# A graph network on one core: one gathered row in each gather is stored to DRAM, and edge step 1 loads its features four steps ahead

## The chip, the cores and the metric

The kernel runs on one core of a Trainium2 chip. The metric is the device time of one execution in microseconds (us). Engines are named as in the profile: PE (matmul; PEld is its weight load), DVE, ACT, POOL and SP. POOL issues the indirect transfers (gathers), SP and ACT issue the ordinary ones; a "q" behind an engine's name stands for its queue of issued transfers.

## The reference

A graph of 12,500 nodes and 412,500 edges, sorted by destination, passes through two networks, each added to x and followed by a layer norm. The first is a two-layer graph convolution. The second, which the change touches, is a mesh network with D = 64 features:

```
n = ln(mlp(node_feat)); e = ln(mlp(edge_feat))
for s in range(2):
    ce = concat([e, n[senders], n[receivers]])
    e  = e + ln(mlp_s(ce))                       # mlp: silu(x @ w0 + b0) @ w1 + b1
    agg = segment_sum(e, receivers)
    n  = n + ln(mlp_node_s(concat([n, agg])))
return mlp(n)
```

## The kernel before, in words

Sorting, the graph convolution and the node encoder run first (to about 5405 us). Then `edge_step(s)` runs twice, for s = 0 (about 5405 to 10757 us) and s = 1 (10777 to 15661 us). Each goes over 405 groups of K = 8 times 128 edges, written out as one straight line of code.

The product of n[senders] with its part of w0 is taken once per node and lies in DRAM as a table, tab_p; n[receivers] as tab_q. Per group:

- `ahead(g)` (L1028) gathers 8 x 128 rows of tab_p on POOL: eight instructions (L407, one per k), each 128 rows of 64 floats, into buffer g % R of `ring`, five buffers pg0 to pg4. It is called LA = 3 groups ahead of the block that reads it, and three times ahead of the loop.
- `send(g)` (L1012) loads, on SP, what the group starts from: in s = 0 the raw edge attributes `at` (L960, two buffers), in s = 1 the edge features e that s = 0 stored (L1018, six buffers).
- `send_window` brings the receivers' window: qd, rows of tab_q (L1045), and rb, relative places (L1041), in four parts. For groups 0 and 1 SP issues them, for all others ACT, between its activations. `hot` (L1050, DVE) turns rb into a one-hot.
- `hidden_enc` (s = 0 only: matmul L965, silu L967) is the edge encoder's first layer. `hidden_blk` adds up in PSUM the product with e and with the one-hot window (L974) and the transposed gathered rows (L976), and ACT takes the silu (L979). `second` (L984, L986) is the second layer, `normalised` the layer norm (DVE L466, L471, and ACT L465), `window_sum` the segment sum (PE L389, then DVE L397).
- s = 0 stores the new e (L1110, SP).

Block g and the parts behind it lie in different steps of the loop (a step is one turn of `for g` in `steps`): in s = 0 encoder, its second layer, its turning, block, second layer and sum are 0 to 5 steps behind, in s = 1 block, second layer and sum 0 to 2. In 25 of the steps a chunk of nodes is updated in between (L926 loads its degrees, L906 and L908 send new tables in s = 0).

The order of PE, DVE and ACT is that of the program text (`manual_schedule`). SP's and POOL's order is the scheduler's, from what each instruction waits for. Engines wait for each other by semaphores. A gather into a ring buffer waits until PE has read the buffer's last contents, five groups before (L976).

Of the kernel before, what the change touches and what calls it, by code (L numbers as in the profile page):

```python
# [9 lines left out]
F32 = mybir.dt.float32  # L10
# [8 lines left out]
P = 128  # L19
K = 8  # L20
W = 64
D = 64
GB = 135
SI, DR = 81, 45
R, LA = 5, 3
# [12 lines left out]
def gcn_then_mesh_gnn_kernel(ctx: ExitStack, tc: tile.TileContext, a: dict, out: bass.AP):  # L38
# [21 lines left out]
    nc = tc.nc  # L60
# [3 lines left out]
    NG = NT // K  # L64
# [6 lines left out]
    KP = K // 2  # L71
    assert N == NB * NP and NB == NCH * CB and NT == IT * TB == ITS * TI

    dram = ctx.enter_context(tc.tile_pool(name="dram", bufs=1, space=bass.MemoryType.DRAM))
# [45 lines left out]
    tabs_p = [dram.tile([N, D], F32, name=f"tab_p{s}") for s in range(2)]  # L120
    tabs_q = [dram.tile([N + 1, D], F32, name=f"tab_q{s}") for s in range(2)]
    tabs_q3 = [dram.tile([N + W, 3, D], BF16, name=f"tab_q3{s}") for s in range(2)]
    e1_d = dram.tile([128, NG * KP * P], F32, name="e1_d")

    def bank(name):
# [84 lines left out]
    with tc.tile_pool(name="sort", bufs=1) as sp, \  # L210
# [7 lines left out]
        k, other = keys  # L218
# [82 lines left out]
        k, free = keys[turn], keys[1 - turn]  # L301
# [102 lines left out]
    def gather(table, idx, to):  # L404

        for k in range(K):
            nc.gpsimd.indirect_dma_start(  # L407
                out=to[:, k, :], out_offset=None, in_=table,
                in_offset=bass.IndirectOffsetOnAxis(ap=idx[:, k:k + 1], axis=0))
# [587 lines left out]
    def edge_step(s):  # L997


        ring = [work.tile([P, K, D], F32, name=f"pg{i}", bufs=1) for i in range(R)]  # L1000
        acc = (s01, 0, 128) if s == 0 else (ns2, D, D)

        ENC, ENC2, TURN, BLK, BLK2, SUM = (0, 1, 2, 3, 4, 5) if s == 0 else (None, None, None, 0, 1, 2)
        CHUNK = 4
        nh = work.tile([D, CN + P - NP], F32, name="nh", bufs=1)
        nc.vector.memset(nh, 0.0)
        feats, hids, hidb, y0, y1, es, windows, hots, ohs, srcs, drls, ny, dh = ({} for _ in range(13))
        col = lambda g: slice(g * KP * P, (g + 1) * KP * P)
        real = lambda g: 0 <= g < NG
        chunk_at = {last_group[c] + SUM + 1: c for c in range(NCH)}  # L1010

        def send(g):  # L1012

            if s == 0:
                feats[g] = edge_inputs(g * KP * P)
            else:
                es[g] = work.tile([128, KP * P], F32, name="e", bufs=6)
                nc.sync.dma_start(es[g], e1_d[:, col(g)])  # L1018

        def send_sources(i):  # L1020
            srcs[i] = work.tile([P, SI * K], I32, name="si")
            nc.sync.dma_start(srcs[i], a["srcT"][:, i * SI * K:(i + 1) * SI * K])

        def send_places(i):
            drls[i] = work.tile([P, DR * K], F32, name="drl")
            nc.sync.dma_start(drls[i], rel_d[:, i * DR * K:(i + 1) * DR * K])

        def ahead(g):  # L1028
            at = g % SI * K
            gather(tabs_p[s], srcs[g // SI][:, at:at + K], ring[g % R])  # L1030

        def send_window(g, eng=nc.sync, parts=range(4)):

            if 0 in parts:
                windows[g] = qd[g % len(qd)], work.tile([128, KP * P], BF16, name="rb", bufs=3)
            q, rb = windows[g]
            for i in parts:
                h = i // 2
                r = slice(h * W, (h + 1) * W)
                if i % 2:  # L1040
                    eng.dma_start(rb[r, :], relg_d[g:g + 1, h, :].to_broadcast([W, KP * P]))  # L1041
                else:
                    at = nc.values_load(base_row[0:1, g:g + 1], engines=[eng.engine], min_val=0, max_val=N,
                                        skip_runtime_bounds_check_because="a destination is a node's number or N")
                    eng.dma_start(q[r, :, h * D:(h + 1) * D], tabs_q3[s][ds(at, W)])  # L1045

        def hot(g):
            q, rb = windows.pop(g)
            ot = work.tile([128, KP * P], BF16, name="ot")
            nc.vector.tensor_scalar(ot, rb, iop, None, op0=OP.is_equal)  # L1050
            hots[g] = [(q[:, i, :], ot) for i in range(3)]

        def steps():
            for g in range(2):
                send(g)
                send_window(g)
            hot(0)
            later = []
            for g in range(NG + SUM + 1 + CHUNK):
                if real(g + 2):  # L1060
                    send(g + 2)
                if g + 8 - SUM >= 0 and real(g + 8 - SUM) and (g + 8 - SUM) % DR == 0:
                    send_places((g + 8 - SUM) // DR)
                if real(g - BLK + LA) and g >= BLK:
                    if (g - BLK + LA + 8) % SI == 0 and real(g - BLK + LA + 8):
                        send_sources((g - BLK + LA + 8) // SI)
                    ahead(g - BLK + LA)

                def window_part(i):
                    if real(g - BLK + 2) and g - BLK >= 0:  # L1070
                        send_window(g - BLK + 2, nc.scalar, [i])


                while later:
                    later.pop(0)()

                if real(g - SUM + 1):
                    c = g - SUM + 1
                    ohs[c] = one_hot(work, drls[c // DR], c % DR)
                if real(g - BLK + 1) and g - BLK >= 0:  # L1080
                    hot(g - BLK + 1)

                parts = []
                if s == 0 and real(g - ENC2):
                    c = g - ENC2
                    y0[c] = work.tile([P, K, D], F32, name="y0", bufs=5)
                    parts.append((second(hids.pop(c), *ee1), y0[c]))
                if real(g - BLK2):
                    c = g - BLK2
                    y1[c] = work.tile([P, K, D], F32, name="y")  # L1090
                    parts.append((second(hidb.pop(c), *eb1[s]), y1[c]))
                if g - 1 in chunk_at:
                    c = chunk_at[g - 1]
                    ny[c] = work.tile([P, CB, D], F32, name="ny", bufs=1)
                    parts.append((node_second(nh, *nb1[s], n=P, name="seg"), ny[c]))
                if parts:
                    normalised(work, P, *parts)
                window_part(0)
                if s == 0 and real(g - TURN):
                    c = g - TURN  # L1100
                    es[c] = work.tile([128, KP * P], F32, name="e", bufs=6)
                    nc.scalar.activation(es[c], turned(y0[c]), AF.Identity, scale=e_g[0])
                window_part(1)
                if real(g - SUM):
                    c = g - SUM
                    y, e = [y1.pop(c)], es.pop(c)
                    if s == 0:
                        later.append(lambda c=c, e=e, pt=turned(y[0]): (
                            nc.vector.scalar_tensor_tensor(e, pt, e_g[1], e, op0=OP.mult, op1=OP.add),
                            nc.sync.dma_start(e1_d[:, col(c)], e)))  # L1110
                        y.insert(0, y0.pop(c))
                    window_sum(ohs.pop(c), base_row, c, lambda k: [v[:, k, :] for v in y], *acc, later)
                if s == 0 and real(g):
                    hids[g] = hidden_enc(feats.pop(g))
                window_part(2)
                if real(g - BLK):
                    c = g - BLK
                    hidb[c] = hidden_blk(s, es[c], ring[c % R], hots.pop(c))
                window_part(3)

                if g in chunk_at:
                    node_hidden(step_products(s, chunk_at[g]), nb_b0[s], nh)
                if g - 2 in chunk_at:
                    c = chunk_at[g - 2]
                    step_update(s, c, node_turned(ny.pop(c)))
                if g - 3 in chunk_at:
                    c = chunk_at[g - 3]
                    if s == 0:
                        send_tables(1, c)
                    else:  # L1130
                        dh[c] = decode_hidden(c)
                if s and g - 4 in chunk_at:
                    c = chunk_at[g - 4]
                    decode_second(c, dh.pop(c))

        with tc.For_i(0, trip_count(0, 1)):
            send_sources(0)
            send_places(0)
            for g in range(LA):
                ahead(g)  # L1140
            with tc.manual_schedule(engines={ET.PE, ET.DVE, ET.Activation}):
                steps()
# [105 lines left out]
```

## Time and profile before

| what | value |
|---|---|
| time, median of 3 runs | 15701.25 us (15689.59 to 15710.15) |
| the profiled execution's own time | 15723.23 us |
| its span | 15721.3 us, 272757 instructions, mean clock 0.827 |
| gathers on POOL (L407) | 6480, 6280.7 us, 969 ns each |
| DMA issues: at, e_d, e | 405 each on SP: 32 KB, 256 KB, 256 KB |
| DMA issues: rb, qd | 1612 each on ACT: 64 KB, 24 KB |
| moved by DMA | 873.80 MB, 56 GB/s over the span |

The profile gives, for each engine, busy time and number of instructions; for a group of instructions, its line, operation, what it writes and reads, count, busy time and mean duration, and then the idle time of the engine just before it with what ended most of it. In the waits, a row reads: engine and line that waited, what released it, total us, times, longest us. "remote" is a release that the profile can't tie to one instruction, "issue" a gap in which the engine waited for nothing that the profile shows. In the timeline a row has start, duration, engine and line, and in brackets the idle time before it.

### The profile page before, as it was taken

The numbers are of one execution on the slowest core, as the hardware profiler recorded it, in microseconds if no ns is written. First come the engines' busy times: TensorE is split into PE (matmuls) and PEld (weight loads), VectorE is DVE, ScalarE is ACT, GpSimd is POOL, SyncE is SP. The second block draws the span as 40 slices with busy tenths as digits, with TensorE's granted clock in tenths as the row PEclk, the third lists the DMA queues.
The fourth block names the chain that finished last, engine by engine and source line by source line (L and its number), as shares of the span: only waits on it lengthen the run. The fifth ranks groups of instructions, "written<-read, shape, count | busy, mean of one in ns | idle before, by whom it ended". The sixth has DMA issues, their size and how long they took to land. (4 is left out here: it accounts for less than half of the span.)

```text
span 15721.3 us, 272757 instructions
## 1 busy us (share of the span) xinstructions
PE 11403.3 (73%) x104441; PEld 8610.0 (55%) x104442; DVE 8828.1 (56%) x22535; ACT 2363.1 (15%) x3705; POOL 6285.8 (40%) x6598
## 2 busy tenths in 40 slices
PE   0086999989997588888888888885665566556565
PEld 0076999879997355555555555553444444444443
DVE  9976777767777355555554555553444344444444
ACT  3400000000000122222222222221111111111111
POOL 0000000000000165555565556654666666666665
PEclk9998999989998588888887878887777777777777
DMA  0002111121111122222222222222222222222222
GB/s 28 0 15 45 65 67 65 55 57 65 66 66 43 40 62 60 61 60 59 60 61 57 59 59 61 59 59 57 60 61 61 59 61 60 60 61 60 60 60 50
DMA packets 1009217, 873.80 MB, mean 56 GB/s; under 512 B 650006, under 2 KB 757370, under 8 KB 1007214
## 3 DMA queue, kind: packets, MB, share of 16 engines
q1 hardware_dynamic: 336256, 497.56, 10.2%
q0 software_dynamic: 207360, 212.75, 8.2%
q10 hardware_dynamic: 464256, 145.47, 3.9%
q8 instruction: 855, 14.01, 0.4%
q14 instruction: 490, 4.01, 0.1%
HBM read 720.51 MB, written 134.51 MB: 54 GB/s over the span
## 5 line engine op out<-in xcount | busy, mean ns | idle before, releaser
L407 POOL DMA_INDIRECT pg<-tab_p,si x6480 | 6280.7, 969 | 8528.9 <-DMA qd<-tab_q 4585.1
L986 PE MATMUL ps_o<-eb_w,h 128*128 128x128 f32 x6480 | 1394.3, 382 | 1809.3 <-ACT h L979 1571.7
L986 PEld LDWEIGHTS ps_o<-eb_w,h 128*128 128x128 f32 x6480 | 1187.9, 275 | 2067.7 <-ACT h L979 1703.9
L598 PE MATMUL ps_h<-t,roh 128*128 128x112 bf16 (+1 forms) x39936 | 2131.2, 211 | 238.0 <-DVE roh L574 238.0
L598 PEld LDWEIGHTS <-roh 128*128 128x128 bf16 x39936 | 2010.3, 98 | 287.5 <-DVE roh L574 241.7
L614 PE MATMUL ps_seg<-ohd,msg 128*112 128x112 f32 (+1 forms) x13312 | 1618.0, 266 | 0.0
L1050 DVE TENSOR_SCALAR ot<-rb,iop 128x512 bf16<-128x512 bf16 x810 | 295.8, 365 | 2347.4 <-DMA rb<-relg_d 1422.5
L466 DVE TENSOR_REDUCE var<-sq 128x8 f32<-128x512 f32 (+2 forms) x1290 | 843.4, 666 | 1305.0 <-issue 739.1
L389 PE MATMUL ps_seg<-oh,y 128*64 128x64 f32 x19440 | 1290.6, 256 | 181.8 <-issue 163.1
L614 PEld LDWEIGHTS ps_seg<-ohd,msg 128*112 128x112 f32 (+1 forms) x13312 | 1406.9, 172 | 0.5
L389 PEld LDWEIGHTS ps_seg<-oh,y 128*64 128x64 f32 x19440 | 1138.5, 166 | 343.8 <-issue 313.0
L605 DVE TENSOR_TENSOR msg<-ps_h,wm 128x448 f32<-128x448 f32 (+1 forms) x1536 | 974.4, 634 | 459.6 <-PE ps_h L598 454.3
L974 PE MATMUL ps_h<-e,eb_w 128*128 128x512 f32 x1620 | 1184.2, 814 | 61.7 <-issue 35.3
L602 DVE TENSOR_TENSOR ohd<-ior,rdrel 128x448 f32<-128x448 f32 (+1 forms) x1536 | 1010.1, 658 | 235.1 <-PE ps_seg L614 235.1
L465 ACT ACTIVATE sq<-ps_o 128x512 f32<-128x512 f32 (+1 forms) x1240 | 735.0, 593 | 2575.7 <-remote 638.2
L979 ACT ACTIVATE h<-ps_h,eb_b 128x512 f32<-128x512 f32 x810 | 556.5, 687 | 3043.4 <-remote 1920.9
L471 DVE TENSOR_TENSOR y<-ps_o,rs_y 128x512 f32<-128x512 f32 x1215 | 802.7, 688 | 85.4 <-issue 0.9
L974 PE MATMUL ps_h<-ot,qd 128*128 128x512 bf16 x2430 | 778.5, 423 | 94.2 <-issue 80.7
L377 DVE TENSOR_TENSOR oh<-iow,drl 128x512 f32<-128x512 f32 x1215 | 829.8, 683 | 12.5 <-DMA drl<-rel_d 5.3
L976 PE MATMUL ps_h<-ident,pg 128*128 128x128 f32 x3240 | 600.8, 296 | 319.4 <-issue 220.0
L986 PE MATMUL ps_o<-ee_w,h 128*128 128x128 f32 x3240 | 640.9, 359 | 223.7 <-ACT h L967 211.2
L986 PEld LDWEIGHTS ps_o<-ee_w,h 128*128 128x128 f32 x3240 | 544.9, 254 | 400.1 <-ACT h L967 324.4
(264 smaller groups left out, 10998.3 us busy)
## 6 DMA issues: line engine op xcount, KB each, us to landing
mod<-mod_d SPq DMA_DIRECT2D x256, 832.0 KB
pg<-tab_p,si POOLq DMA_INDIRECT x6480
e_d<-e SPq DMA_DIRECT2D x405, 256.0 KB
e<-e_d SPq DMA_DIRECT2D x405, 256.0 KB
rb<-relg_d ACTq DMA_DIRECT2D x1612, 64.0 KB
qd<-tab_q ACTq DMA_DIRECT2D x1612, 24.0 KB
at<-in_attrT SPq DMA_DIRECT2D x405, 32.0 KB
tab_q<-tabs SPq DMA_DIRECT2D x50, 187.5 KB
```

The costliest lines, as they stand in the source:

```text
L377: nc.vector.tensor_tensor(oh, iow[:, None, :].to_broadcast([P, K, W]), drl[:, g * K:(g + 1) * K, None].to_broadcast([P, K, W]), op=OP.is_e ...
L389: nc.tensor.matmul(ps[r:r + n, :W], v, oh[:, k, :], start=(k == 0), stop=(k == K - 1))
L407: nc.gpsimd.indirect_dma_start(out=to[:, k, :], out_offset=None, in_=table, in_offset=bass.IndirectOffsetOnAxis(ap=idx[:, k:k + 1], axis=0))
L465: nc.scalar.activation(sq, o.rearrange("p (k f) -> p k f", f=D), AF.Square, scale=D ** -0.5)
L466: nc.vector.tensor_reduce(v[:, i:i + k], sq, axis=AX.X, op=OP.add)
L471: nc.vector.tensor_tensor(y, o, r[:, i:i + k, None].to_broadcast(list(y.shape)), op=OP.mult)
L598: nc.tensor.matmul(pg[:, (j - j0) * sb * F:(j - j0 + 1) * sb * F], ohs[h][:, u, at * P:(at + 1) * P], t3[:, i, u, b:b + sb * F], start=(i ...
L602: nc.vector.tensor_tensor(ohd[:, :n, :], ior[:, None, :].to_broadcast([P, n, LR]), drel[:, j0:j0 + n, r:r + 1].to_broadcast([P, n, LR]), o ...
L605: nc.vector.tensor_tensor(msg[:, :n * sb * F].rearrange("p (j s f) -> p j s f", s=sb, f=F), pg[:, :n * sb * F].rearrange("p (j s f) -> p j ...
L614: nc.tensor.matmul(acc[:sb * F, :LR], msg[:, j * sb * F:(j + 1) * sb * F], ohd[:, j, :], start=(j0 + j == packs[0][0]), stop=((j0, n, sb) ...
L974: nc.tensor.matmul(ph, w, v, start=(i == 0), stop=False)
L986: nc.tensor.matmul(po[:, j * 128:(j + 1) * 128], h[:, j * P:(j + 1) * P], w1, start=False, stop=(j == KP - 1))
```

## The change

After the eight gathers of a group, `ahead(g)` issues eight DMAs on SP, each storing the row that the k-th gather brought to partition 0 (64 floats, 256 bytes) into a new DRAM tensor, seen_d. Nothing reads seen_d. Over both steps these are 6480 stores. In s = 1 `send` runs LA + 1 = 4 groups ahead instead of 2, and e has 8 buffers instead of 6; in s = 0 it stays 2. The first loads of a step are now all issued before the first windows, in both steps. No arithmetic changes.

```diff
+    seen_d = dram.tile([2 * NG, K, D], F32, name="seen_d")
...
         CHUNK = 4
+        LOAD = 2 if s == 0 else LA + 1
...
             else:
-                es[g] = work.tile([128, KP * P], F32, name="e", bufs=6)
+                es[g] = work.tile([128, KP * P], F32, name="e", bufs=LOAD + 4)
                 nc.sync.dma_start(es[g], e1_d[:, col(g)])
...
         def ahead(g):
             at = g % SI * K
             gather(tabs_p[s], srcs[g // SI][:, at:at + K], ring[g % R])
+            for k in range(K):
+                nc.sync.dma_start(seen_d[s * NG + g:s * NG + g + 1, k, :], ring[g % R][0:1, k, :])
...
         def steps():
+            for g in range(LOAD):
+                send(g)
             for g in range(2):
-                send(g)
                 send_window(g)
             hot(0)
             later = []
             for g in range(NG + SUM + 1 + CHUNK):
-                if real(g + 2):
-                    send(g + 2)
+                if real(g + LOAD):
+                    send(g + LOAD)
```

## The prediction

> **What bounds the kernel now.** I read the page first, then busy time by stage, then the waits of one stage, then a few steps of the timeline.
>
> ```profile
> PE 11403.3 (73%) x104441; PEld 8610.0 (55%) x104442; DVE 8828.1 (56%) x22535; ACT 2363.1 (15%) x3705; POOL 6285.8 (40%) x6598
> ...
> L407 POOL DMA_INDIRECT pg<-tab_p,si x6480 | 6280.7, 969 | 8528.9 <-DMA qd<-tab_q 4585.1
> ```
>
> No engine is full over the span. POOL does nothing but issue the 6480 gathers, all inside the two edge steps. So I split the busy time by stage (5405 to 10757 us is edge step 0, 10777 to 15661 us edge step 1):
>
> ```profile
> 5405.00:10757.00 5352.00, 4378.71 (x28512) 2780.51 (x28512) 2737.69 (x8329) 1355.13 (x2095) 3144.39 (x3240) 0.82 0.26 59
> 10777.00:15661.00 4884.00, 2895.56 (x14462) 1991.16 (x14462) 1963.99 (x7002) 556.12 (x882) 3136.28 (x3240) 0.74 0.28 60
> ```
>
> (Columns: length, PE, PEld, DVE, ACT, POOL busy, clock, DMA share, GB/s.) A step of 405 lasts 13.2 us in stage 0 and 12.06 us in stage 1. In stage 1 PE is busy 59%, POOL 64%, the DMA engines 28%. Nothing saturates, so a loop of waits sets the step. The waits from 11000 to 15000 us, and then SP's own:
>
> ```profile
> ACT h L979 <- remote: 1578.1, 217, 9.6
> ...
> POOL pg L407 <- issue: 714.6, 2343, 0.6
> POOL pg L407 <- remote: 554.6, 233, 3.6
> ```
>
> ```profile
> SPq L1018 <- remote: 2771.8, 204, 18.7
> SPq L1018 <- PE ps_h L974: 289.2, 45, 17.0
> ```
>
> ACT waits long before the silu L979, whose input is PE's L976; POOL pauses once per group, because the five gather buffers are a ring and gather g+5 must wait for PE's L976 of block g; SP mostly sleeps. One step:
>
> ```profile
> 13082.63 0.94 POOL L407 DMA_INDIRECT pg<-tab_p,si  x1 [2.04 <-remote]
> ...
> 13088.92 0.60 PE L976 MATMUL ps_h<-ident,pg 128*128 128x128 f32 x4
> ...
> 13091.36 0.94 POOL L407 DMA_INDIRECT pg<-tab_p,si  x1 [0.30 <-issue]
> 13094.30 0.23 DVE L397 TENSOR_TENSOR ns<-ns,ps_seg 64x64 f32 x1 [4.18 <-remote]
> ...
> 13094.59 0.69 ACT L979 ACTIVATE h<-ps_h,eb_b 128x512 f32<-128x512 f32 x1 [8.58 <-remote]
> ...
> 13094.66 1.39 POOL L407 DMA_INDIRECT pg<-tab_p,si  x1 [2.36 <-remote]
> ```
>
> L976 is recorded as done at 13089.52, yet its reader L979, the DVE add L397 and the next gather all start together at 13094.3 to 13094.7, about 2 us after the eighth gather instruction was issued (13091.36 + 0.94 = 13092.30). In the steps I looked at, that gather's last packet lands some 1.2 us after issue, and PE's results become visible 0.6 to 0.8 us after that, several at once. So a step is 8 x 1.247 us of gather issue (0.94 + 0.30), 1.2 us of landing, 0.75 us until PE's results are seen, 0.1 us more: 12.0 us, as observed. Why the results are seen so late, the trace doesn't say (ends of matmuls are modelled); that they follow the gather in flight is what matters here.
>
> **The change, part by part.** All sums are made on the profiled execution: span 15721.3 us, 15723.2 us with what lies around it. That is 22 us (0.14%) above the median of the runs, 15701.25; I add the difference to the median.
>
> *POOL.* As the scheduler places the code, every gather also waits for the store of the same buffer five groups earlier, some 60 us old: satisfied. If the extra wait costs an instruction, half the gathers of before carry such a wait already (POOL's EVENT_SEMAPHORE, 17 ns), and their spacing is the same 1.247 us. Cost 0; upper bound 17 ns x 8 = 0.14 us a step, 110 us over 810.
>
> *SP's issue time.* 16 x 405 = 6480 stores of one 256-byte row. No SP store of that size is in the trace; the nearest rows are its other issues, 0.23 us (a 2 KB load) to 0.37 us (the 256 KB store):
>
> ```profile
> 8009.75 0.33 SPq L960 DMA_DIRECT2D at<-in_attrT  x1
> 8010.17 0.37 SPq L1110 DMA_DIRECT2D e_d<-e  x1
> 8021.94 0.33 SPq L960 DMA_DIRECT2D at<-in_attrT  x1
> ```
>
> SP issues two transfers 0.42 us apart, without waiting for the first to land, then sleeps 11.8 us. Eight stores add 8 x 0.42 = 3.4 us of issue to a queue with over 11 us free per step: hidden. The Trainium skill speaks against the change here ("DMA: Bandwidth & Descriptors", "Anatomy of one DMA" and "Rules for kernel authors"): each DMA has a fixed cost of about 2 us, mostly the write receipt from memory, and many small transfers should be merged. Were the eight served one behind another, that is 16 us a step, longer than the step: about +4 us x 810 = +3,200 us. By the row it is latency behind an issue of 0.4 us, and nobody reads seen_d. I take the row; the 2 us return below as the age of a store that someone waits for.
>
> *What is queued behind a waiting store.* Each store waits on SP for its gather to land. SP's order in stage 0 is: stores k0 to k6 of the gather in flight, the load `at` (L960), store k7, the e1 store (L1110). `at` needs PE's L965, which is seen in the same late burst, 0.75 us after k7 has landed, and k6 lands 1.25 us before k7. So the stores in front have cleared about 2 us before `at` may go: cost 0; without that cover each us would push `at`, which has most of a step until L965 wants it. In stage 1 all eight stores stand before the load of e. It is not late now, and the change asks for it four groups ahead with eight buffers instead of two with six; a buffer still comes from the group four steps back. It trails by at most a step and has several: cost 0. The cn, si, drl and table transfers (25 chunks) stand between stores too and may be held 1 us each: +10 us, bounds 0 and 25.
>
> *ACT's window loads.* DMAs of SP and ACT share eight completion counters in turn, so a load waits for the DMA eight before it, which is now often a store. In stage 0 the third and fourth window loads wait for stores k2 and k3 of the gather in flight. k3 is issued by POOL at 3 x 1.247 + 0.94 = 4.7 us into the gather, lands at 5.9, its store goes at 6.2; a small transfer's last byte here came 1.0 us after issue (cn, 2 KB, issued 8027.05, landed 8028.0), the skill's figure is 2 us: done at 7.2 to 8.2. ACT gets to that load at about 11.8, after the silu: margin 3.6 us or more. In stage 1 the first three loads wait for stores k4, k6, k7 of the gather before, k7 landed at 13082.63 - 2.04 + 1.2 = 13081.8 in the step shown, so its store is done by 13084.2, and ACT comes to that load at 13087.69: margin 3.5 us. Cost 0; a rival has the other end.
>
> *DMA engines.* 6480 packets of 256 bytes and as many of 4. A 4-byte packet takes 0.01 us, a 2 KB packet about 0.1; so at most 0.1 x 6480 / 16 = 41 us per engine, 0.3% of the span, at 28% load. What counts is only a delay of the k7 landing: at most one packet of 0.1 us, by chance on one of sixteen engines. I take 0.02 us x 810 = +16 us; bounds 0 and 80.
>
> *Stage starts.* Three groups are gathered ahead of the loop, so 24 stores stand in SP's queue before the second window of group 0 and all of group 1. POOL began at 5410.78; its 24th gather is issued at 5439.64 + 0.94 and lands at 5441.8, where before SP sent the last of those windows at 5415.10. The first one-hot (DVE L1050) moves from about 5414 to 5444. Before, the first L976 was dispatched 26 us after that one-hot and its result was seen at 5467.6; now 5444 + 26 = 5470, and seen between 5470 and the same lateness again, 28 us. POOL meanwhile fills its ring, 40 instructions, until 5461. I take +15 us for stage 0 (bounds 2 and 31) and, with the same layout but e loads sent first, +5 for stage 1 (0 to 20).
>
> Sum: 10 + 16 + 15 + 5 = +46 us on 15723; on the median 15,747, say 15,745. Bounds of this case: 15,690 to 15,850.
>
> **The rivals.**
> *The late burst is relieved (faster).* If PE's results are seen late because of the way POOL's gathers run unanswered, an engine that answers each gather may change that. For: lateness of 5 us in L976 is no work of PE. Against: ACT issues three transfers inside that step (13085.9 to 13087.7) and they relieve nothing; PE's L976 already waits on gathers. Price: then the step is POOL's own, 10.0 us of issue and 0.3 to 0.4 of turning round, 10.4 (some steps of stage 1 do run at 10.4): 405 x (12.06 - 10.4) = -670 us. In stage 0 PE is busy 4378.7 / 405 = 10.8 us a step, so perhaps 12: 405 x 1.2 = -490. In full 14,540; at half 15,120, which I give as its time.
>
> *ACT is held by a store's counter (slower).* Place: the window loads at L1041 and L1045, ahead of ACT's next silu and squares. It decides when a store ends more than 3.5 us later than reckoned, for instance because SP itself sat on a store whose own counter belongs to an ACT load not yet issued. Each us beyond costs 810 us in both stages; half a us on average gives 15,745 + 405 = 16,150. For: the coupling is in the order of both queues. Against: the margins above.
>
> *Nothing measurable.* The start delays vanish in the ring and the packets hit nothing: 15,701, the lower part of my own case.
>
> **How the numbers follow.** My case 0.45 (of it 0.25 slower by over 0.2%, 0.20 within), relieved burst 0.30, held ACT 0.25. 0.2% is 31 us, about what a measurement of this kernel can tell. So faster 0.30, same 0.20, slower 0.50. The range reaches into both rivals, until a tenth is left out at each end: 15,000 (more than half of the relief) to 16,400 (0.8 us of hold a step). The likeliest case alone is 15,690 to 15,850.
>
> **What would show it.** Right: POOL's gathers still 1.247 us apart, its pause per group 2 to 3 us, stage 1 steps near 12 us, the first L979 of stage 0 some 15 us later than 5468.75. Relief: L979 starting within 2 us of L976 in mid-gather, pauses of 0.3 us, PE clock above 0.74 in stage 1. Held ACT: new waits of ACT on DMAs seen_d before L1041 or L1045, and longer pauses on POOL. The prediction fails if a store's latency is several us, if SP falls behind its step, or if the hold of PE's results depends on who waits for a gather.

## The result, and the profile after

The changed kernel takes 16576.38 us (median of 4 runs, 16572.64 to 16581.1) against 15695.42 us before: ratio 1.0566, 95% interval 1.0546 to 1.0585. That is 881 us more where 45 were forecast, outside the range. One fact is needed to read the later numbers: the kernel before takes 13,710 us on four of the five chips that the experiments met, and 15,704 us on the fifth. The recorded measurement looks like the fifth. I call the four free chips and the other a holding chip, for a reason that the traces give below; ratios are only formed between runs on one chip.

The page of the changed kernel:

```profile
PE 11807.0 (71%) x104441; PEld 8713.4 (53%) x104442; DVE 8836.8 (53%) x22535; ACT 2364.3 (14%) x3705; POOL 6263.8 (38%) x6598
...
L408 POOL DMA_INDIRECT pg<-tab_p,si x6480 | 6258.7, 966 | 9407.2 <-DMA at<-in_attrT 4590.3
```

PE's busy time rose by 404 us with the same 104441 instructions; DVE's, ACT's and POOL's did not. By stage (edge step 0 now ends at 11508, edge step 1 runs from 11555 to 16516 us; columns as in the prediction):

```profile
5405.00:11508.00 6103.00, 4761.47 (x28512) 2855.19 (x28510) 2741.01 (x8328) 1355.97 (x2095) 3089.28 (x3239) 0.76 0.21 52
11555.00:16516.00 4961.00, 2913.79 (x14450) 2015.38 (x14450) 1964.03 (x6987) 556.07 (x881) 3167.91 (x3240) 0.74 0.24 59
```

From the starts of the silu L979 (now L980) the 853 us between the two spans fall apart as follows: edge step 0's mean step went from 13.09 to 14.95 us (404 steps, +750), edge step 1's from 11.98 to 12.15 (+66), the passage from one stage to the next from 62 to 100 us (+37), the start of edge step 0 from 5468.75 to 5469.96 (+1), and what follows the last silu fell by 1. The question is the 750. In stage 0 PE's busy time rose by 383 us (4378.71 to 4761.47) while the granted clock fell from 0.82 to 0.76: by PE's own account half of the loss is the same work at a slower clock, the other half PE standing idle for longer. This account doesn't say which of the two brings the other about.

SP's waits from 12000 to 16000 us (the part of them that is on record) show some of the sleep that the prediction counted on, now shared between the load of e (L1020, mostly "remote") and the stores, which wait for the gathers (L1034):

```profile
SPq L1020 <- remote: 697.1, 195, 7.0
SPq L1034 <- DMA pg<-tab_p,si: 360.3, 240, 4.7
```

One step of edge step 0; the prediction's timeline showed one of edge step 1:

```profile
7736.24 0.95 POOL L408 DMA_INDIRECT pg<-tab_p,si  x1 [0.31 <-issue]
...
7738.20 1.04 PE L995 MATMUL ps_t<-ident,y 128*128 128x128 f32 x8
...
7738.99 3.56 SPq L1034 DMA_DIRECT2D seen_d<-pg  x4
7739.17 0.92 PE L390 MATMUL ps_seg<-oh,y 128*64 128x64 f32 x24
...
7741.05 0.22 PE L390 MATMUL ps_seg<-oh,y 128*64 128x64 f32 x1 [0.95 <-issue]
...
7741.77 0.22 PE L390 MATMUL ps_seg<-oh,y 128*64 128x64 f32 x1 [0.51 <-issue]
7742.51 0.95 POOL L408 DMA_INDIRECT pg<-tab_p,si  x1 [0.30 <-issue]
7743.19 0.27 PE L390 MATMUL ps_seg<-oh,y 128*64 128x64 f32 x1 [1.20 <-issue]
7744.59 0.69 ACT L1107 ACTIVATE e<-ps_t,e_g 128x512 f32<-128x512 f32 x1 [5.29 <-remote]
...
7745.76 2.07 PE L966 MATMUL ps_h<-at,ee_w 16*128 16x512 f32 x2
7747.76 2.08 PE L975 MATMUL ps_h<-e,eb_w 128*128 128x512 f32 x2
...
7751.60 0.95 POOL L408 DMA_INDIRECT pg<-tab_p,si  x1 [8.15 <-PE ps_h L977]
```

Read it from PE. L995 (the turning) is dispatched by 7739.2; its reader on ACT, L1107, starts at 7744.59, 1.1 us after the issue of the last gather instruction ended (7742.51 + 0.95). PE dispatches 24 products of the segment sum L390 and then stops in the midst of them: four single products, 0.5 to 1.2 us idle before each, and "issue" means that they wait for nothing recorded. Only when the gather is through does PE run on, and then with L966, L975 and L977 still to do, at half clock (granted 0.5 from 7743.09 on, after PE had been idle): 6 us more, so POOL pauses 8.15 us. A common step of edge step 0 before looks otherwise:

```profile
8004.66 1.29 PE L389 MATMUL ps_seg<-oh,y 128*64 128x64 f32 x32
...
8007.00 0.94 POOL L407 DMA_INDIRECT pg<-tab_p,si  x1 [0.31 <-issue]
8007.90 0.81 PE L974 MATMUL ps_h<-ot,qd 128*128 128x512 bf16 x3
8009.47 0.64 PE L976 MATMUL ps_h<-ident,pg 128*128 128x128 f32 x4 [0.76 <-DMA pg<-tab_p,si]
...
8010.09 1.26 POOL L407 DMA_INDIRECT pg<-tab_p,si  x1 [2.15 <-PE ps_h L976]
```

When the last gather has been issued (at 8007.94), PE has L389 and L965 behind it and is in L974; only L976 is left, and POOL pauses 2.15 us.

Both kinds of step are in both traces. Before, POOL's pause in edge step 0 is under 2.5 us in 270 of 404 steps, which last 12.1 us at a mean granted clock of 0.87, and over 5 us in 73, which last 17.0 us at 0.70 (the rest lie between). After, 46 are of the short kind (12.2 us, 0.88) and 215 of the long one (16.6 us, 0.72). The two kinds differ in where PE is when the last gather of the group has been issued: still in L389 or L965 in 58 of the 73 long steps and in none of the 270 short ones (after: 206 of the 215, and none of the 46). So the hold of PE, and its long form, were there before; what changed is how often it catches PE early in its work: in 72 steps before and 258 after. The groups of PE where it stops, before and after (times from 5405 us on; the last part is idle time just ahead of the group and what ended it):

```profile
L389 PE MATMUL ps_seg<-oh,y 128*64 128x64 f32 x19440 | 1290.6, 256 | 181.8 <-issue 163.1 <-DVE x L952 13.1 <-DVE y L471 4.2
L974 PE MATMUL ps_h<-e,eb_w 128*128 128x512 f32 x1620 | 1184.2, 814 | 61.7 <-issue 35.3 <-DMA qd<-tab_q 23.3
...
L976 PE MATMUL ps_h<-ident,pg 128*128 128x128 f32 x3240 | 600.8, 296 | 319.4 <-issue 220.0 <-DMA pg<-tab_p,si 95.4
...
L965 PE MATMUL ps_h<-at,ee_w 16*128 16x512 f32 x810 | 508.2, 698 | 102.9 <-issue 88.4 <-DMA qd<-tab_q 12.2 <-DMA rb<-relg_d 0.6
```

```profile
L390 PE MATMUL ps_seg<-oh,y 128*64 128x64 f32 x19440 | 1409.4, 255 | 647.9 <-issue 617.9 <-DVE x L953 24.4 <-DVE y L472 4.4
L975 PE MATMUL ps_h<-e,eb_w 128*128 128x512 f32 x1620 | 1346.3, 915 | 166.2 <-issue 138.1 <-DMA e<-e_d 24.4
...
L966 PE MATMUL ps_h<-at,ee_w 16*128 16x512 f32 x810 | 650.2, 855 | 320.9 <-issue 266.1 <-DMA seen_d<-pg 36.4 <-DMA qd<-tab_q 12.2
L977 PE MATMUL ps_h<-ident,pg 128*128 128x128 f32 x3240 | 632.4, 327 | 81.5 <-issue 68.3 <-DMA pg<-tab_p,si 12.4
```

PE stands idle for 789 us more ahead of L390, L975 and L966 (466 + 105 + 218), nearly all of it "issue", and for 238 us less ahead of L977, the last products of a block: its stops moved forward in the step. The mean durations of L975 and L966 rose with the slower clock (814 to 915 ns, 698 to 855). Over all of stage 0, PE's stops of over 0.5 us that the profile calls "issue" went from 450 (440 us) to 1026 (1063 us).

### The profile page after: what moved, and what is told of

It is laid out like the page before. It is cut to its first block, busy times and chain, and to the rows that moved or that the text cites. A ratio compares the mean times of both kernels' runs of the same rounds, so it can differ in the third digit from the quotient of the medians.

```text
span 16574.5 us, 289246 instructions
## 1 busy us (share of the span) xinstructions
PE 11807.0 (71%) x104441; PEld 8713.4 (53%) x104442; DVE 8836.8 (53%) x22535; ACT 2364.3 (14%) x3705; POOL 6263.8 (38%) x6598
## 5 line engine op out<-in xcount | busy, mean ns | idle before, releaser
L987 PE MATMUL ps_o<-eb_w,h 128*128 128x128 f32 x6480 | 1351.6, 373 | 1870.6 <-ACT h L980 1689.6
L987 PEld LDWEIGHTS ps_o<-eb_w,h 128*128 128x128 f32 x6480 | 1150.8, 267 | 2112.2 <-ACT h L980 1800.6
L390 PE MATMUL ps_seg<-oh,y 128*64 128x64 f32 x19440 | 1409.4, 255 | 647.9 <-issue 617.9
L390 PEld LDWEIGHTS ps_seg<-oh,y 128*64 128x64 f32 x19440 | 1192.7, 166 | 785.4 <-issue 746.4
L975 PE MATMUL ps_h<-e,eb_w 128*128 128x512 f32 x1620 | 1346.3, 915 | 166.2 <-issue 138.1
L980 ACT ACTIVATE h<-ps_h,eb_b 128x512 f32<-128x512 f32 x810 | 556.6, 687 | 4190.7 <-remote 2610.6
L975 PE MATMUL ps_h<-ot,qd 128*128 128x512 bf16 x2430 | 909.2, 487 | 197.1 <-issue 178.1
L975 PEld LDWEIGHTS <-qd 128*128 128x128 bf16 x2430 | 293.8, 122 | 1138.2 <-issue 1078.4
L966 PE MATMUL ps_h<-at,ee_w 16*128 16x512 f32 x810 | 650.2, 855 | 320.9 <-issue 266.1
L977 PEld LDWEIGHTS ps_h<-ident,pg 128*128 128x128 f32 x3240 | 527.0, 176 | 352.8 <-issue 261.9
```

What stands on the lines that cost most here:

```text
L390: nc.tensor.matmul(ps[r:r + n, :W], v, oh[:, k, :], start=(k == 0), stop=(k == K - 1))
L975: nc.tensor.matmul(ph, w, v, start=(i == 0), stop=False)
L987: nc.tensor.matmul(po[:, j * 128:(j + 1) * 128], h[:, j * P:(j + 1) * P], w1, start=False, stop=(j == KP - 1))
```

## The experiments

The theories. **1**: the waits. Stores wait on SP for the gather in flight, and what is queued behind them is late. **2**: the number. Eight more small transfers beside each gather lengthen PE's hold. **3**: the counters that SP's and ACT's transfers share. A start theory (SP's queue is blocked when a stage begins) and theories B, C, P and H are named where they were put. Unless said otherwise an edit is to the changed kernel.

### On free chips: parts of the change

**e1_load_only**: no stores.

```diff
-            for k in range(K):
-                nc.sync.dma_start(seen_d[s * NG + g:s * NG + g + 1, k, :], ring[g % R][0:1, k, :])
```

> The change without its stores: only the earlier loads of e in edge step 1 and the order of the first loads. Theory A (SP's stores, each waiting for its gather, or the transfers themselves, cause the loss in edge step 0): 15,690 to 15,730, as before. Theory B (the longer lead of the e loads causes part of it): edge step 1 alone is longer, +60 to +100 us, so 15,760 to 15,800.

Measured 13711.42 us against 13710.06 before: ratio 1.0000 (0.9992 to 1.0009). The earlier loads cost and bring nothing on this chip, and theory B falls for it. And here the kernel before itself turned out to take 13,710 us.

**e2_stores_s0**: stores in edge step 0 only, loads as before.

```diff
-        LOAD = 2 if s == 0 else LA + 1
+        LOAD = 2
...
-            for k in range(K):
-                nc.sync.dma_start(seen_d[s * NG + g:s * NG + g + 1, k, :], ring[g % R][0:1, k, :])
+            if s == 0:
+                for k in range(K):
+                    nc.sync.dma_start(seen_d[s * NG + g:s * NG + g + 1, k, :], ring[g % R][0:1, k, :])
```

> Stores in edge step 0 only, loads as before. If the loss belongs to edge step 0 by itself (1.86 us a step in the trace of the changed kernel), 15,695 + 750 = 16,445, and edge step 1 back at 12.0 us a step. If the tail of stage 0 or the stage change carries it, less than 16,200.

Measured 13751.24 us, 1.0028 (1.0018 to 1.0039): +41 us. As this is a free chip, it says nothing of the 750.

**e3_merged**: one store of the eight rows.

```diff
-            for k in range(K):
-                nc.sync.dma_start(seen_d[s * NG + g:s * NG + g + 1, k, :], ring[g % R][0:1, k, :])
+            nc.sync.dma_start(seen_d[s * NG + g:s * NG + g + 1], ring[g % R][0:1])
```

> One 2 KB store per group, of all eight rows, waiting for the same eight gathers. Theory 1 (what is queued behind a waiting store on SP is late): the wait for the last gather stays, so most of the loss stays, about 16,300 or more. Theory 2 (the number of transfers, eight more in each gather): an eighth of it, 15,750 to 15,850. Theory 3 (ACT's loads and SP's stores take turns on the same completion counters): nearly gone, about 15,700 to 15,750.

Measured 13755.79 us, 1.0032 (1.0022 to 1.0042): +46.

**e4_const**: eight stores of a constant row.

```diff
-                nc.sync.dma_start(seen_d[s * NG + g:s * NG + g + 1, k, :], ring[g % R][0:1, k, :])
+                nc.sync.dma_start(seen_d[s * NG + g:s * NG + g + 1, k, :], ident[0:1, :D])
```

> Eight stores per group as in the change, but of a constant tile, so that no store waits for a gather (seen_d holds a row of the identity, not gathered rows). Theory 1 (waiting stores on SP): back to 15,700 to 15,760. Theory 2 (number of transfers): as the changed kernel, 16,400 to 16,600. Theory 3 (counters): the counters are shared as before but the stores are older when someone waits for them, so most of the loss is gone, below 15,900.

Measured 13710.19 us, 0.9999 (0.9990 to 1.0008): nothing. On these chips the number of stores costs nothing and one wait per group costs nearly all of the small loss.

**r1_after**, **r2_const**, **r3_merged**: the changed kernel, e4 and e3 again, on another chip, also a free one.

> The changed kernel itself, again, beside the kernel before on the same chip. Where the kernel before takes about 15,700 us, 16,570 again. Where it takes about 13,710, as in the first set of experiments, PE's results are not seen late and POOL never pauses; then the part that stays is the start of the stages and some SP pacing: 13,750 to 13,770, a ratio of 1.003 to 1.005 instead of 1.057.

> Eight stores per group of a constant row (seen_d holds no gathered rows). Where the kernel before takes 15,700: theory 1 (stores that wait for the gather in flight) 15,700 to 15,800; theory 2 (number of transfers beside the gather) 16,400 to 16,600. Where it takes 13,710: 13,710 as in e4_const.

> One 2 KB store per group of all eight rows. Where the kernel before takes 15,700: theory 1 (a store that waits for the gather in flight) 16,300 or more; theory 2 (number of transfers) 15,750 to 15,850. Where it takes 13,710: 13,755 as in e3_merged.

Measured 13770.13 (1.0048, 1.0031 to 1.0064), 13711.13 (1.0002, 0.9994 to 1.0011) and 13757.37 us (1.0036, 1.0022 to 1.0050). The change costs 60 us there. Its stages on the free chip:

```profile
5465.00:9554.00 4089.00, 3566.16 (x28057) 2407.21 (x28460) 2686.14 (x8285) 1340.87 (x2087) 3066.02 (x3200) 0.94 0.34 77
9642.00:13710.00 4068.00, 2695.97 (x14236) 1857.17 (x14439) 1944.33 (x6982) 556.48 (x880) 3061.37 (x3208) 0.78 0.32 71
```

A step is 10.1 us in both stages, POOL pauses 0.3 us between groups as between any two gathers, and PE has 0.94 of its clock in stage 0. PE's signals are free as well: in the trace of before, 396 of the 397 steps of edge step 0 that last under 20 us have more than 3 us without any signal of PE, in the median from 4.2 to 11.7 us after the gather's start; in r2_const it is 16 of 404, in r1_after 92. That is why I call the chips holding and free. A part of this silence may be of the record alone: in edge step 0 the trace of before holds 81% of PE's and 36% of DVE's signals, that of r2_const 95% and 96%. Over both edge steps the six traces from holding chips hold 31 to 37% of DVE's signals, those of e1, h2, r1, r2 and f4 97 to 99%; ahead of the edge steps none of DVE's is missing on either. What does not rest on recorded signals is when instructions start: POOL's pause of 3.2 us a group in the mean before, and ACT's late silu. The landing is no different: the last packet of a group's gathers ends 1.2 us after the end of issue on both kinds of chip.

The 60 us have a visible place. In e4_const a block's silu starts on average 4.0 us (edge step 0) and 2.6 us (edge step 1) after its group's last gather was issued; in r1_after 38.6 and 33.8 us. POOL still runs without a pause, so the lag costs only at the end of a stage, when POOL is through and the blocks are not: 41.4 instead of 11.4 us in stage 0, 29.3 instead of 10.1 in stage 1, together +49. The lag comes with stores that wait (it is 34.6 and 24.6 us in r3_merged, 4.1 and 2.5 in r2_const). The waits of ACT show by what way, here from 10000 to 13500 us in r1_after and then in r2_const:

```profile
ACT h L980 <- DMA rb<-relg_d: 1078.6, 154, 10.6
ACT h L980 <- DMA seen_d<-pg: 661.9, 90, 11.0
```

```profile
ACT h L980 <- PE ps_h L977: 2086.1, 309, 8.8
```

In r2_const the silu waits for PE. In r1_after ACT stands before its window loads, which lie ahead of the silu in its program. By the counters that SP and ACT share, a window load waits for an earlier transfer: an earlier window load, or now a store that itself waits for a gather. The time for which ACT stands (stops of over 0.3 us) before an instruction that waits for such a counter comes to 1431 us in stage 0 and 1769 us in stage 1 of r1_after, to 71 and 3 us in r2_const, and to 1 and 30 us in the recorded changed kernel. So on a free chip the prediction's rival of the held ACT did come, at a small price because POOL has three groups of lead; on the holding chip it did not. This speaks for theory 3 on a free chip; no run changes the counters alone.

**e5_pool_rest**: the kernel before, with memsets on POOL.

```diff
                 in_offset=bass.IndirectOffsetOnAxis(ap=idx[:, k:k + 1], axis=0))
+            if rest is not None and k % 2:
+                nc.gpsimd.memset(rest, 0.0)
```

> The kernel before, with a memset of a spare tile on POOL after every second gather (four per group). It tests what holds back PE's results. Theory H (a run of gathers without a pause on POOL holds them, and a pause lets them out): where the kernel before takes 15,700 the step is shorter than 12 us in spite of some 0.3 us more per memset, 15,000 or less. Rival (they wait for the landing of the last gather, pauses or not): 4 x 0.3 us more a step, 15,700 + 970 = 16,670. Where the kernel before takes 13,710 and POOL never pauses, the memsets only add: 14,700.

Measured 14762.6 us, 1.0771 (1.0753 to 1.0789). As a test of the hold it failed twice: the chip was a free one, and in stage 0 the memsets do not lie between the gathers of a group (9.82 us from first to last, as without them). POOL's row says what it did measure:

```profile
L411 POOL MEMSET rest<- 128x256 f32 x3240 | 1040.2, 321 | 4745.4 <-DMA tab_q<-tabs 4579.8 <-DVE nh L1009 55.6
```

1,040 us of work on POOL made the kernel 1,052 us longer: there POOL is the bound.

**f1_stores_s1** (stores only `if s == 1`) and **f2_not_first** (stores only `if g >= LA`).

> Stores in edge step 1 only, loads as in the change. Start theory (SP sends the first windows of a stage only behind the stores of the first three groups): where the kernel before takes 13,710, +20 to +30 us from the start of edge step 1 alone and 10.1 us a step. Where it takes 15,700: +66 from longer steps and +37 from the start, as the two traces show, about 15,800. Rival (edge step 1 is hurt by the stores through its e loads): 10.3 us a step or more, +80.

> The changed kernel without the stores of the first three groups of each stage (24 of 3240 rows are not stored), so that SP's queue is free when the first windows are due. Start theory: where the kernel before takes 13,710, the loss falls from 60 us to 10 or less. Rival (every group costs a little): still 50 to 60. Where the kernel before takes 15,700 both give 16,500, since the loss there is in each step of edge step 0.

f1: 13734.2 us, 1.0017 (1.0010 to 1.0024), +24, with 10.08 us a step, as the start theory had it. But f2: 13771.41 us, 1.0041 (1.0027 to 1.0055), still +61. The first silu of stage 0 came earlier, at 5444.8 instead of 5464.8 us, and the stage ended at the same time (9551.6 and 9554.0). Edge step 1 likewise began at 9613 instead of 9642 us and ended at 13710 in both. The start theory fell; the lag above replaced it.

**f3_stores16** and **f4_stores32**: each row stored two and four times (the diff is that of f3; f4 has 4 for 2; seen_d grows with it).

```diff
-            for k in range(K):
-                nc.sync.dma_start(seen_d[s * NG + g:s * NG + g + 1, k, :], ring[g % R][0:1, k, :])
+            for k in range(2 * K):
+                nc.sync.dma_start(seen_d[s * NG + g:s * NG + g + 1, k, :], ring[g % R][0:1, k // 2, :])
```

> Each row stored twice, to two places: 16 stores a group. Cover theory (SP's issue of 0.42 us each is hidden while it is less than a step): 6.7 us of issue a step, so no more than the changed kernel plus the start, 13,770 to 13,800 where before takes 13,710; rival (each transfer costs the step something): 60 us become 120. Where before takes 15,700, theory 2 (more transfers hold PE's results longer) gives over 17,000.

> Each row stored four times: 32 stores a group, 32 x 0.3 to 0.42 = 10 to 13.4 us of SP's issue, plus about 0.8 for its other transfers: SP is the bound or nearly. Where before takes 13,710: at 0.42 us each 14.2 us a step, 17,000; at 0.31 us 10.7 us a step, 14,250. It says which is the price of one when the cover is gone.

f3: 13786.47 us, 1.0057 (1.0040 to 1.0074): +77 where the changed kernel had +60 on another free chip, so eight more stores a group cost some 16 us in all. The lag is smaller than in r1_after (28.7 and 11.0 us), but the step of stage 0 grew to 10.21 us; more stores are not simply more lag. f4: 17521.6 us, 1.2777 (1.2756 to 1.2799), with 14.68 us a step in stage 0: 32 stores, `at` and the e1 store are 34 transfers of SP, 0.43 us each if the step is divided by them. But that is not the price of an issue. Where SP does not wait, its transfers follow each other every 0.30 us (the median spacing), and 34 of them make 10 us, about POOL's own step; in a quarter of stage 0 (1488 of 5931 us) SP stands still, mostly for the counters of ACT's window loads. From 6000 to 9000 us:

```profile
SPq L1034 <- DMA qd<-tab_q: 272.8, 286, 3.1
SPq L1034 <- DMA rb<-relg_d: 249.6, 179, 3.3
```

ACT in turn stands 2345 us of stage 0 before instructions that wait for counters. The cover is real and ends between 16 and 32 stores; what ends it is SP's issue time together with the two queues waiting for each other.

### On a holding chip: PE made to wait

g1 to g4 shorten the ring to four and let PE really wait for the newest gather, by a product with zeros that reads its last rows and adds nothing to the result.

```diff
-R, LA = 5, 3
+R, LA = 4, 3
...
             nc.tensor.matmul(ph, w, v, start=(i == 0), stop=False)
+        if newest is not None:
+            nc.tensor.matmul(ph[:, :D], zeros, newest, start=False, stop=False)
         for j in range(KP):
```

g1 is the kernel before with it, g2 the changed kernel, g3 the changed kernel with constant rows (so g2 and g3 have the earlier loads too, which differ from before in edge step 1 and at the start of a stage); in g4 (from the kernel before) the product stands behind the encoder's, in edge step 0 only:

```diff
-        nc.tensor.matmul(ph, ee_w0, at, start=True, stop=True)
+        nc.tensor.matmul(ph, ee_w0, at, start=True, stop=newest is None)
+        if newest is not None:
+            nc.tensor.matmul(ph[:, :D], zeros, newest, start=False, stop=True)
```

> The kernel before with a ring of four and, just ahead of each block's transposed gather rows (L976), a product of zeros with the newest gather's last rows: PE's block and POOL's next gather now wait for each other. Expected in both steps: 9.8 us of gathers, 1.2 of landing, about 1.5 to 2.5 until the next gather starts, so 12.5 to 13.5 us a step, 15,600 to 16,400 in all, a rhythm like that of the recorded trace of before.

> The changed kernel with the same ring and extra product. Theory C (SP's order and the shared counters cost time once the step is a loop of gather and block): 1.9 us a step more than g1 in edge step 0, +700 or more. Theory P (they cost nothing; the loss of the recorded run comes from where PE's own work is held): within 100 us of g1.

> As g2, but the stores are of a constant row and wait for no gather (seen_d holds a row of the identity). Theory C: near g1, since no store waits. Theory P: near g1 too; if it were as slow as g2 while g2 is slow, the number of transfers would be the cause.

> The kernel before with a ring of four and the extra product at the encoder's matmul (L965) instead, in edge step 0 only: the wait for the newest gather then lies ahead of L965, L974 and L976. Theory P: that work, about 3 us at full clock and 6 at half, comes on top of the landing: 14 to 16 us a step in edge step 0, as in the recorded trace of the changed kernel, against 12.5 to 13.5 in g1. If it is not slower than g1, the place of the hold doesn't matter.

This chip was a holding one: the kernel before took 15704.06 us. The four on one chip, with the mean step of each stage from the silu's starts:

| kernel | us | ratio to before (95%) | step in stage 0 | stage 1 |
|---|---|---|---|---|
| g1_late | 16258.13 | 1.0350 (1.0333 to 1.0368) | 13.83 | 12.40 |
| g3_late_const | 16652.94 | 1.0594 (1.0577 to 1.0612) | 14.89 | 12.47 |
| g2_late_stores | 16901.65 | 1.0753 (1.0729 to 1.0778) | 15.50 | 12.46 |
| g4_late_enc | 16692.33 | 1.0625 (1.0607 to 1.0643) | 15.49 | 11.96 |

g1 met its range in all (15,600 to 16,400), though neither stage lies within its 12.5 to 13.5 us a step. The rhythm of the recorded pair is back: g2 is 643 us slower than g1, 1.67 us a step of edge step 0 and 0.06 of edge step 1 (recorded: 1.86 and 0.16). Neither C nor P is right as put: P fails by its number, C by its reason. Constant rows, for which no store waits, already cost 395 of the 643 us (1.06 us a step); that the stores read gathered rows and wait for them adds 249 (0.61). The same constant rows cost nothing on three free chips, there with the ring of five and without the extra product. Stage 0 of g1, then g3, then g2:

```profile
5456.00:11045.00 5589.00, 4581.06 (x29262) 2921.23 (x29262) 2738.73 (x8293) 1350.66 (x2087) 3065.76 (x3207) 0.80 0.25 56
```

```profile
5464.00:11480.00 6016.00, 4862.96 (x29263) 3034.03 (x29262) 2735.43 (x8285) 1351.20 (x2087) 3055.15 (x3208) 0.77 0.23 53
```

```profile
5466.00:11728.00 6262.00, 4991.02 (x29262) 3113.92 (x29261) 2743.75 (x8287) 1351.26 (x2087) 3049.70 (x3208) 0.75 0.22 51
```

The same number of PE's instructions, clock 0.80, 0.77, 0.75, busy time up by 282 of the 427 us and then 128 of the 246 us by which the stage grew: both parts of the recorded loss, more of it busy time in g3 than there. PE's "issue" stops rise too, from 554 (502 us) in g1 to 837 (797 us) in g3 and 1030 (1039 us) in g2, and so do the steps of edge step 0 in which the end of the gathers' issue finds PE still in its segment sum or its encoder: 149, 231, 242.

g4 shows that the place of the wait matters: with it ahead of L965, L974 and L976 a step of stage 0 is 15.49 us, 1.66 more than in g1, and POOL's pause 5.8 us (g1: 4.1; recorded changed kernel: 5.2). That was theory P's figure, 14 to 16.

**h1_const**, **h2_merged**: e4 and e3 once more, on a fourth free chip.

> The change with eight stores per group of a constant row, none waiting for a gather (seen_d holds a row of the identity). Where the kernel before takes 15,700: theory 2 (number of transfers beside the gather) 16,150 to 16,400, most of the 880 us, as in g3; theory 1 (stores waiting for the gather) 15,700 to 15,800. Where it takes 13,710: 13,710 again.

> The change with one 2 KB store per group that waits for all eight gathers. Where the kernel before takes 15,700: theory 2 an eighth to a quarter of the loss, 15,800 to 15,900; theory 1 16,300 or more. Where it takes 13,710: 13,755 again.

Measured 13709.41 us (0.9995, 0.9986 to 1.0005) and 13746.41 us (1.0024, 1.0014 to 1.0034), as before.

## Why the prediction was wrong, point by point

- **What bounds the kernel.** Right for this chip: a loop of gather, landing, PE's late results and the next gather. Wrong was the sentence that went with it, that why the results are late need not be known. I carried 0.75 us from landing to PE's results over as a constant. It could be one only as long as PE had dispatched its whole step by the time it was held, as in the step that I showed. That step was of edge step 1. The sum of 12.0 us never fitted edge step 0, whose 13.1 us (mean pause 3.2, not 2 to 2.4) I left unexplained: 73 of its pauses were already over 5 us.
- **The failed step: DMA engines.** The working said that what counts of 6480 small transfers is only a delay of the last gather's landing, 16 us, bounds 0 to 80, with PE's lateness behind the landing held at 0.75 us. The landing was not delayed (its last packet ends 1.13 us after the end of issue in edge step 0, 1.21 before). What grew is the lateness, and it took about 750 us: PE is held before it is through L390, its remaining products then run behind the gather, and after the idle time at half clock. That the number of transfers alone does this is shown for the holding chip with the altered ring (395 of 643 us, constant rows); for the recorded kernels themselves it is the likeliest reading, not shown. By what path the transfers make PE be caught earlier stays open.
- **POOL.** Right: the gathers of a group take 9.81 us in stage 0 (9.90 before), 9.99 in stage 1 (9.88). The pause per group was forecast at 2 to 3 us; it is 5.2 in stage 0 (3.2 before) and 2.2 in stage 1.
- **SP's issue time, and the rule of 2 us for each transfer.** Right: hidden at 8 stores a group and nearly so at 16. A store's issue takes 0.21 us, and stores without a wait follow each other every 0.30 us (f4), so 0.42 us was on the high side. The row was the better guide than the rule's sum of +3,200 (about 2,700 with edge step 0's own 13.2 us). The section of the Trainium skill that the prediction takes the 2 us from ("DMA: Bandwidth & Descriptors", "Anatomy of one DMA") is on transfers that GpSimd issues; these are SP's.
- **What is queued behind a waiting store.** Put at 0; on free chips the waiting stores make the greater part of the 60 us, since the blocks end a stage 30 and 19 us later behind POOL. It costs once a stage, not in each step.
- **The rival of the held ACT.** On the holding chip it did not come: ACT stands before a counter of the transfers for 1 us in stage 0 and 30 us in stage 1 of the recorded changed kernel. On a free chip it came (1431 and 1769 us), against the margins of 3.5 us that I gave, and cost little only because POOL sets the step there.
- **Stage starts.** Stage 0 started 1 us later, not 15; stage 1 37 us later, not 5. f2 showed, on a free chip, that the mechanism was the wrong one.
- **The rival of the relieved burst.** The change relieves nothing: the hold became worse. But its price was no fancy: on a free chip, with no hold, both kernels run at POOL's 10.1 us a step, and 13,710 is even less than the 14,540 worked out. And there the forecast of +46 us would have been near (+60), but by luck: most of the 60 us come from the waits that it put at 0.
- The early warning in the prediction's last sentence (it fails if the hold of PE's results depends on who waits for a gather) named the right place, but I gave it no case among the slower ones.

What stays open: what differs between the chips, and whether the loss of records on the holding one is a companion of the hold or has a part in it; by what path small transfers make the hold catch PE earlier; and whether merged or constant stores would save the recorded kernel, since neither met a holding chip with the ring of five.

## What to carry to other kernels

Where a trace shows an engine's results arriving later than its work, and the reason is not known, that lateness is not a constant to build a sum on: price what happens if it grows, and look how much of the engine's work would then lie behind it. Do this for every stage: the one step that was read fitted its sum, and the loss came in the stage whose steps did not. An engine with idle time is not free of cost when the idle time moves: in the step shown PE came back from it to a granted clock of 0.5, and the mean clock of the long steps is 0.70 to 0.72, that of the short ones 0.87 to 0.88. And transfers that wait for nothing cost 395 us on one chip and nothing on three others (though with another ring), so a change of this kind has to be timed on more than one.

## What the runs showed of the hardware

- One program, 13,710 us on four chips and 15,704 on a fifth, each within 0.7%. On the fifth PE's results are taken up only after the gather in flight has landed, several at once, and PE stops in products that wait for nothing recorded (450 stops of over 0.5 us in edge step 0 of the recorded kernel before); there is one such stop in r1_after and none in r2_const. The traces of holding chips also lack most of DVE's signals. What makes a chip one or the other is not in these traces.
- The ordinary transfers of SP and ACT take turns on eight counters, so a store that waits for a gather can hold a later transfer on either queue: ACT stands 1431 and 1769 us in the two stages of r1_after, and SP a quarter of stage 0 in f4.
- On the holding chip a step of edge step 1 hardly grows with the stores (0.06 to 0.16 us), one of edge step 0 by 1.67 to 1.86: behind the second layer, a step of stage 0 has 51 products and transposes of PE to send until the block is complete (8 of L995, 32 of L390, 2 of L966, 5 of L975, 4 of L977), one of stage 1 has 25. That this difference is the reason was not tested by itself; g4 and the two kinds of step speak for it.
